# A graph layer: columns of an on-chip x picked by VectorE for one of four gathers in each 16th run, with a sliding window of node sums

## The chip, the cores and the metric

The kernel runs on one core of a Trainium2 chip. All times are device microseconds of that core. The kernel before took 3992.48 us (median of three runs, 3992.14 to 3996.18). The profile is one more execution, taken by the hardware profiler.

## The reference

A graph with 12,500 nodes of 128 features and 412,500 edges, sorted by their destination. Features 0 to 31 are scalars, the other 96 are 32 vectors of three. For each edge an MLP of the 8 edge scalars gives four sets of 32 weights. The features of the source node are multiplied by the weights and by the edge's attributes, summed over the edges of each destination, projected, mixed with a product of the node's own features, added to x, and normalised along the features:

```python
f0 = x0 @ W1_0e / np.sqrt(MUL);  f1 = jnp.einsum('nui,uw->nwi', x1, W1_1o) / np.sqrt(MUL)
feat0, self0 = f0[:, :MUL], f0[:, MUL:];  feat1, self1 = f1[:, :MUL], f1[:, MUL:]
e0, e1 = feat0[edge_src], feat1[edge_src]
h = gelu(gelu(ea8 @ W_mlp1 / np.sqrt(8)) @ W_mlp2 / np.sqrt(64))
w00, w01, w10, w11 = h @ Wp_00, h @ Wp_01, h @ Wp_10, h @ Wp_11
...
mid0, mid1 = ...
n0 = segment_sum(mid0, edge_dst) / np.sqrt(32);  n1 = segment_sum(mid1, edge_dst) / np.sqrt(32)
y0 = c * self0 + s * (n0 @ W2_0e / np.sqrt(64));  y1 = ...
out = layernorm(x + concatenate([y0, y1]))
```

## The kernel before

The edges are cut into 806 runs of 512 (four columns q of 128 edges each) and the runs into 202 chunks of four. The order of work is written out by hand in the main loop over s (lines 717 to 761) for TensorE, ScalarE, VectorE and SP. GpSimd has the gathers alone.

- Prologue (lines 673 to 716). Each of 25 groups of 512 nodes is loaded, transposed into `acc` (`turn`, L187 to L192), multiplied by the feature weights `wf` (`features_of`, L194) and stored in DRAM as `table`. The first 16 runs don't wait for the table: they gather rows of x, which `turn_rows` (L414) and `features` (L422) turn into features on chip.
- `gather(s)` (L119 to L126). Four indexed DMAs on GpSimd, each bringing 128 rows of 512 bytes into `G[s]`. `G` has LEAD = 20 buffers, and the gathers of run s + 19 are issued in step s, so a gather waits until the messages 20 runs back have read their buffer.
- `aid(s, t)` (L108 to L117). In every 14th run from 36 on (55 runs) the last column isn't gathered by GpSimd: SP loads row numbers into registers, 16 at a time, and issues 128 single-row DMAs, beginning 16 steps ahead.
- `weights`, `mlp1`, `mlp2`, `radial`: the edge MLP on TensorE and ScalarE, a chunk at a time.
- `messages(s)` (L444, L447): VectorE multiplies the weights (in PSUM) by the gathered features into `M`. It stands in VectorE's order ahead of `placing(s)` (`pl`, L465), and in step 2 of a chunk ahead of `add`.
- `segments(s - 1)` (L456): TensorE sums the messages over up to 32 nodes of a column with the selection matrix `S` (`select`, L431 and L435, once a chunk). ScalarE copies the sums out (`sg`, L459).
- `place`, `project` (L472, L473, L481): TensorE puts the four runs of a chunk in node order and multiplies them by the output weights.
- `add(c)` (L485 to L490): VectorE loads four node numbers from `first_node` into registers and adds four 128x32 blocks to `acc` at those columns. `acc` holds all 12,500 nodes, transposed; it begins as x, so the residual is in it from the start.
- `self_part(b)` (L493 to L501): for each group, x is loaded again, transposed, multiplied by `ws` and added to `acc`. The 25 groups are spread over the first quarter of the loop.
- `norm(bs)` (`moments`, L506 to L524; `normalise`, L526 to L544): a group whose nodes are complete (`due`, L264 to L268) is transposed out of `acc`, normalised and stored.
- `general()` is a slow path for inputs that don't fit the fixed windows. It isn't entered for these inputs.

The lines on which the order around the change rests:

```python
G[s] = wk.tile([P, Q, P], F32, name="G", bufs=LEAD)
for q in range(Q - 1 if s in aided else Q):
...
if s + LEAD - 1 < NS:
    gather(s + LEAD - 1)
...
if 0 < s <= NS:
    segments(s - 1)
...
if s < NS:
    messages(s)
    placing(s)
```

Of the kernel before, what the change touches and what calls it, by code (L numbers as in the profile page):

```python
# [24 lines left out]
Q = 4  # L25
# [13 lines left out]
CATCH_UP = 46  # L39
MARGIN = 64  # L40
AID = 14
# [3 lines left out]
STEPS = 12  # L45
LNB = 2
# [3 lines left out]
def gnn_kernel(ctx: ExitStack, tc: tile.TileContext, x, src, dst, ea4, ea8, w1_0, w1_1, wm1, wm2,  # L50
# [44 lines left out]
    G, Y = {}, {}  # L95
    aided = range(AID_FROM, NS - 1, AID)
    assert AID_FROM >= raw_runs and AID_LEAD < LEAD and P % ROWS == 0 and STEPS <= AID
    assert len(aided) <= P

    aid_rows = cst.tile([max(len(aided), 1), P], I32)  # L100
    aid_at = cst.tile([max(len(aided), 1), P], I32)

    def aid_load():

        nc.sync.dma_start(aid_rows, sub(src, AID_FROM * SB + (Q - 1) * P, [[AID * SB, len(aided)], [1, P]]))
        nc.vector.tensor_scalar(aid_at, aid_rows, float(4 * P), None, op0=OP.mult)

# [11 lines left out]
    def gather(s):  # L119
        b, c = divmod(s, P)  # L120
        G[s] = wk.tile([P, Q, P], F32, name="G", bufs=LEAD)
        for q in range(Q - 1 if s in aided else Q):
            rows = idx_raw[:, s, q:q + 1] if s < raw_runs else idx[b][:, q, c:c + 1]
            nc.gpsimd.indirect_dma_start(  # L124
                out=G[s][:, q, :], out_offset=None, in_=x if s < raw_runs else table,
                in_offset=bass.IndirectOffsetOnAxis(ap=rows, axis=0))  # L126
# [14 lines left out]
    acc = cst.tile([P, N + W], F32)  # L141
# [45 lines left out]
    def turn(b):  # L187
        n0, nn, full, tail, tiles = group(b)
        PX[b] = ps.tile([P, GN], F32, name="w", bufs=CH)
        for t, k in tiles:  # L190
            nc.tensor.transpose(PX[b][:, t * P:t * P + k], XT[b][:k, t, :], ident[:k, :k])
        nc.scalar.activation(acc[:, n0:n0 + nn], PX[b][:, :nn], AF.Copy)  # L192

    def features_of(b):  # L194
        n0, nn, full, tail, tiles = group(b)
        pf = ps.tile([P, XB, P], F32, name="w", bufs=CH)
        for t, k in tiles:
            nc.tensor.matmul(pf[:k, t, :], acc[:, n0 + t * P:n0 + t * P + k], wf, start=True, stop=True)
        PF[b] = wk.tile([P, XB, P], F32, name="ft", bufs=3)
        if full:  # L200
            nc.vector.tensor_copy(PF[b][:, :full, :], pf[:, :full, :])
        if tail:
            nc.vector.tensor_copy(PF[b][:tail, full, :], pf[:tail, full, :])
# [15 lines left out]
    def clear():  # L219
        nc.vector.memset(wpost, 0.0)  # L220
        nc.vector.memset(acc[:, N:], 0.0)
        nc.vector.memset(ones, 1.0)
        nc.vector.memset(odd, 0.0)
# [20 lines left out]
    def make_ws():  # L244
        keep = math.cos(MIX) / math.sqrt(MUL)
        nc.vector.memset(ws, 0.0)
        nc.vector.tensor_scalar(ws[:MUL, :MUL], w1[:MUL, MUL:], keep, None, op0=OP.mult)
        nc.vector.scalar_tensor_tensor(ws[:, MUL:].rearrange("p (c i) -> p i c", i=3),
                                       comp[:, :, None].to_broadcast([P, 3, MUL]), keep,
                                       w1[:, None, MUL:].to_broadcast([P, 3, MUL]), op0=OP.mult, op1=OP.mult)  # L250

# [10 lines left out]
    self_from = min(raw_runs + CATCH_UP, NS // 4)  # L262
    self_every = max(1, (NS // 4) // NG)
    due = {}  # L264
    for b in range(NG):
        c = math.ceil((min((b + 1) * GN, N) + MARGIN) / N * NCH) - 1
        c = max(c, (self_from + self_every * (b + 1)) // CH)
        due.setdefault(min(c, NCH - 1), []).append(b)  # L268
    floor = cst.tile([1, NS], F32)

    def set_floor():
        nc.vector.memset(floor, 0.0)
        for c, bs in due.items():
            if (c + 1) * CH < NS:
                nc.vector.memset(floor[:, (c + 1) * CH:], float((bs[-1] + 1) * GN))

# [206 lines left out]
    def add(c):  # L483
        ns = min(CH, NS - c * CH)
        _, at = nc.values_load_multi_w_load_instructions(  # L485
            first_node[0:1, c * CH:c * CH + ns], engines=[DVE], min_val=0, max_val=N - 1,
            skip_runtime_bounds_check_because="node numbers")
        for k in range(ns):
            a = acc[:, bass.ds(at[k], W)]
            nc.vector.tensor_tensor(a, PC[c][:, k, :], a, op=OP.add)  # L490

    def self_part(b, xt):
        n0, nn, full, tail, tiles = group(b)  # L493
        pt = ps.tile([P, GN], F32, name="m", bufs=1)
        for t, k in tiles:
            nc.tensor.transpose(pt[:, t * P:t * P + k], xt[:k, t, :], ident[:k, :k])
        xs = wk.tile([P, GN], F32, name="xs", bufs=1)
        nc.scalar.activation(xs[:, :nn], pt[:, :nn], AF.Copy)
        pf = ps.tile([P, GN], F32, name="h")
        nc.tensor.matmul(pf[:, :nn], ws, xs[:, :nn], start=True, stop=True)  # L500
        nc.vector.tensor_tensor(acc[:, n0:n0 + nn], pf[:, :nn], acc[:, n0:n0 + nn], op=OP.add)  # L501
# [4 lines left out]
    def moments(b):  # L506
# [8 lines left out]
        st = wk.tile([P, XB, 6], F32, name="bst")  # L515
        for t, k in tiles:
            nc.tensor.transpose(pt[:k, t, :], acc[:, n0 + t * P:n0 + t * P + k], ident)
# [29 lines left out]
    def norm(bs, last=False):  # L547
        for b in bs:
            moments(b)
            if len(pend) == LNB:  # L550
# [5 lines left out]
    def general():  # L556
        T = max(t for t in range(1, P + 1) if E % t == 0)
        weight = dr.tile([NS, SB], F32)
        sums = dr.tile([N + P, P], F32)
        for b in range(NB):  # L560
            ns = min(P, NS - b * P)
            raw = load_run_rows(dst, b, NO_NODE)
            f = wk.tile([P, SB], F32, name="rawf")
            g = wk.tile([P, SB], F32, name="rawr", bufs=1)
            nc.vector.tensor_copy(f[:ns, :], raw[:ns, :])
            against_window(f, g, ns)
            nc.vector.tensor_scalar(f[:ns, :], g[:ns, :], 0.0, None, op0=OP.is_lt)
            nc.vector.tensor_scalar(g[:ns, :], g[:ns, :], J - 0.5, None, op0=OP.is_ge)
            nc.vector.tensor_tensor(f[:ns, :], f[:ns, :], g[:ns, :], op=OP.add)
            nc.sync.dma_start(weight[b * P:b * P + ns, :], f[:ns, :])  # L570
# [10 lines left out]
        wcol = weight.rearrange("s e -> (s e)")[:E].rearrange("(n t) -> t n", t=T)  # L581
# [4 lines left out]
        with tc.For_i(0, E // T, 1) as i:  # L586
            si = wk.tile([T, 1], I32, name="g_si")
            di = wk.tile([T, 1], I32, name="g_di")
            we = wk.tile([T, 1], F32, name="g_we")
# [4 lines left out]
            nc.sync.dma_start(we, wcol[:, bass.ds(i, 1)])  # L594
            nc.sync.dma_start(a4, r4[:, bass.ds(i, 1), :].rearrange("t n k -> t (n k)"))
            nc.sync.dma_start(a8, r8[:, bass.ds(i, 1), :].rearrange("t n k -> t (n k)"))
            g = wk.tile([T, P], F32, name="g_g", bufs=1)
            nc.gpsimd.indirect_dma_start(out=g, out_offset=None, in_=table,
                                         in_offset=bass.IndirectOffsetOnAxis(ap=si, axis=0))
            nc.vector.tensor_scalar(a4, a4, we, None, op0=OP.mult)  # L600
            p0 = ps.tile([RAD, T], F32, name="m", bufs=1)
            nc.tensor.transpose(p0, a8, ident[:T, :T])
            t8 = wk.tile([RAD, T], F32, name="g_t8", bufs=1)
# [3 lines left out]
            h1 = wk.tile([HID, T], F32, name="g_h1", bufs=1)  # L607
# [3 lines left out]
            h2 = wk.tile([HID, T], F32, name="g_h2", bufs=1)  # L611
# [3 lines left out]
            w = wk.tile([T, P], F32, name="g_w", bufs=1)  # L615
            nc.scalar.activation(w, pw, AF.Copy)

            m = wk.tile([T, 4, P], F32, name="g_m", bufs=1)
# [14 lines left out]
            mt = wk.tile([P, 4, P], F32, name="g_mt", bufs=1)  # L633
# [4 lines left out]
            y = wk.tile([T, P], F32, name="g_y", bufs=1)  # L638
# [6 lines left out]
            eq = wk.tile([T, T], F32, name="g_eq", bufs=1)  # L645
# [3 lines left out]
            eb = wk.tile([T, T], F32, name="g_eb", bufs=1)  # L649
# [6 lines left out]
            old = wk.tile([T, P], F32, name="g_old", bufs=1)  # L656
            nc.gpsimd.indirect_dma_start(out=old, out_offset=None, in_=sums,
                                         in_offset=bass.IndirectOffsetOnAxis(ap=di, axis=0))
            new = wk.tile([T, P], F32, name="g_new", bufs=1)
# [3 lines left out]
        for b in range(NG):  # L663
            n0, nn, full, tail, tiles = group(b)
            xt = load_nodes(b, sums)
            pt = ps.tile([P, GN], F32, name="m", bufs=1)
            for t, k in tiles:
                nc.tensor.transpose(pt[:, t * P:t * P + k], xt[:k, t, :], ident[:k, :k])
            nc.vector.tensor_tensor(acc[:, n0:n0 + nn], pt[:, :nn], acc[:, n0:n0 + nn], op=OP.add)
        norm(range(NG), last=True)  # L670

    with tc.manual_schedule(engines={PE, ACT, DVE, SP}):
# [35 lines left out]
        selfs, loaded = list(range(NG)), {}  # L708
# [7 lines left out]
        set_floor()  # L716
        for s in range(NS + 1 + CH):
# [13 lines left out]
            if k == 0 and c + 1 < NCH:  # L731
                mlp2(c + 1)
# [8 lines left out]
            if 0 < s <= NS:  # L741
                segments(s - 1)
            if k == 1 and 0 < c <= NCH:
# [13 lines left out]
            if selfs and s + 8 >= self_from and (s + 8) % self_every == 0:  # L757
                b = selfs.pop(0)
                loaded[s + 8] = b, load_nodes(b)
            if s in loaded:  # L760
                self_part(*loaded.pop(s))
        assert not selfs and not loaded


    late = cst.tile([1, NS], F32)
    nc.vector.tensor_copy(late, first_node)
    nc.vector.tensor_tensor(late, late, floor, op=OP.is_lt)
    nc.vector.tensor_reduce(odd[0:1, 2 * NB:], late, axis=mybir.AxisListType.X, op=OP.add)
# [35 lines left out]
```

## Time and profile before

| what | value |
|---|---|
| median of the timed runs | 3992.48 us |
| the profiled execution, its own time | 6014.41 us |
| its span, first to last instruction | 6012.6 us |
| TensorE clock granted, mean | 0.671 |
| TensorE busy | 3220.7 us (54%) |
| GpSimd busy | 2992.1 us (50%) |
| VectorE busy | 1693.3 us (28%) |
| ScalarE busy | 1024.6 us (17%) |
| gathers issued by GpSimd | 3105 from the table, 64 from x |
| single-row DMAs issued by SP | 7040 |
| packets in the span | 1,011,283 (265.85 MB, 44 GB/s) |

The profiled execution is 2022 us longer than the timed ones, so its shares of busy time are not those of a timed run. The table of groups gives, for each line of code and kind of instruction, the count, the busy time, the mean of one in ns, and the idle time of its engine just before it with what ended most of it. "PE" is TensorE, "PEld" its weight loads, "DVE" VectorE, "ACT" ScalarE, "POOL" GpSimd; a "q" behind the name is that engine's sequencer. The timeline gives start and length in us, engine, line, operation and tiles, and in brackets the idle time before it and what ended it. "remote" stands for a release that the profile can't name, "issue" for no wait that it shows.

### The profile page before, as it was taken

To read this page: it belongs to the slowest core of one execution; us is meant where nothing else is said; L and a number is where in the kernel's file an instruction comes from. 1 tells how busy PE (TensorE), PEld (TensorE's weight loads), DVE (VectorE), ACT (ScalarE), POOL (GpSimd) and SP (SyncE) were. 2 spreads that over 40 slices of the span, in tenths; PEclk is the share of its full clock that TensorE was granted. 3 is DMA by queue.
4 is the path that set the end of the run, shared out by engine and by line. 5 is a ranking of instruction groups with operands and counts; after the bars stand their busy time and mean duration, and the time that the engine had idled before them with its cause. 6 is when DMAs were issued, how large, how long until landed. Compare 5 with 4: busy or idle time off the path is not lost.

```text
span 6012.6 us, 82144 instructions
## 1 busy us (share of the span) xinstructions
PE 3220.7 (54%) x25199; PEld 2267.2 (38%) x25199; DVE 1693.3 (28%) x4943; ACT 1024.6 (17%) x2262; POOL 2992.1 (50%) x3176
## 2 busy tenths in 40 slices
PE   3654555555556555555555454545465455555446
PEld 3433433343334333333433333334343333343334
DVE  2322322222322222322222232222233222232223
ACT  1211111121111111111111111112112111111112
POOL 4555444544445545554554455454555555455552
PEclk6766666666766666666666666666666666666667
DMA  5222222222222222222222222222222222222221
GB/s 123 45 40 47 42 46 45 43 49 47 44 48 43 42 41 46 41 42 40 39 40 43 43 40 44 40 42 42 44 40 43 42 40 43 41 41 41 43 41 23
DMA packets 1011283, 265.85 MB, mean 44 GB/s; under 512 B 901422, under 2 KB 958519, under 8 KB 1010833
## 3 DMA queue, kind: packets, MB, share of 16 engines
q0 software_dynamic: 101408, 207.89, 13.4%
q1 hardware_dynamic: 889167, 46.16, 9.2%
q10 hardware_dynamic: 20258, 6.46, 0.4%
q8 instruction: 201, 3.29, 0.2%
q14 instruction: 249, 2.04, 0.1%
HBM read 247.45 MB, written 12.80 MB: 43 GB/s over the span
## 4 chain that ended last, share of the span: by engine, by line
PE 24%; another core or an unknown queue 23%; issue 5%; ACT 5%; DVE 2%; SPq 0%; DVEq 0%; DMA 0%; ACTq 0%
PE seg L456 4%; PE w L405 4%; PE m L473 4%; PE m L481 4%; PE m L472 3%; PE h L388 3%; PE h L373 2%; ACT h L393 1%; ACT h L377 1%; ACT sg L459 1%; ACT y L542 0%; PE m L364 0%; DVE M L447 0%; DVE acc L490 0%
## 5 line engine op out<-in xcount | busy, mean ns | idle before, releaser
L124 POOL DMA_INDIRECT G<-table,idx x3105 | 2930.6, 944 | 2910.9 <-DVE pl L465 1470.7
L456 PE MATMUL seg<-M,S 128*32 128x256 f32 x6448 | 667.5, 491 | 1845.4 <-ACT sg L459 1479.0
L465 DVE TENSOR_SCALAR pl<-iota,colv 128x128 f32<-128x128 f32 x806 | 227.2, 282 | 2441.6 <-PE m L473 2181.3
L456 PEld LDWEIGHTS seg<-M,S 128*32 128x32 f32 x6448 | 144.1, 122 | 2008.9 <-ACT sg L459 1526.5
L459 ACT ACTIVATE sg<-seg 128x256 f32<-128x256 f32 x806 | 310.6, 385 | 3143.1 <-remote 1978.9
L447 DVE TENSOR_TENSOR M<-w,G 128x384 f32<-128x384 f32 x1580 | 798.6, 547 | 0.0
L405 PE MATMUL w<-wpb,h 64*128 64x128 f32 x6448 | 693.5, 373 | 16.1 <-issue 15.9
L405 PEld LDWEIGHTS w<-wpb,h 64*128 64x128 f32 x6448 | 588.6, 267 | 154.8 <-issue 151.0
L388 PE MATMUL h<-h,w2b 64*64 64x256 f32 x3232 | 365.4, 473 | 351.8 <-ACT h L377 318.1
L473 PE MATMUL m<-pl,sg 128*128 128x96 f32 x1612 | 550.0, 442 | 0.0
L481 PE MATMUL m<-st,wpost 128*128 128x128 f32 (+1 forms) x1616 | 388.9, 416 | 146.9 <-ACT st L475 133.2
L472 PEld LDWEIGHTS m<-pl,sg 128*128 128x128 f32 x1612 | 404.8, 308 | 164.6 <-issue 117.0
L490 DVE TENSOR_TENSOR acc<-m,acc 128x32 f32 x806 | 154.5, 192 | 1072.8 <-PE m L481 402.4
L472 PE MATMUL m<-pl,sg 128*128 128x32 f32 x1612 | 424.3, 355 | 10.7 <-ACT eT L366 5.9
L473 PEld LDWEIGHTS m<-pl,sg 128*128 128x128 f32 x1612 | 413.3, 314 | 0.0
L481 PEld LDWEIGHTS m<-st,wpost 128*128 128x128 f32 x1616 | 335.8, 308 | 192.8 <-ACT st L475 141.7
L444 DVE TENSOR_TENSOR M<-w,G 128x256 f32<-128x256 f32 x790 | 330.3, 418 | 227.2 <-remote 218.2
L388 PEld LDWEIGHTS h<-h,w2b 64*64 64x64 f32 x3232 | 159.8, 158 | 542.1 <-ACT h L377 456.1
L393 ACT ACTIVATE h<-h 128x512 f32<-128x512 f32 x404 | 226.6, 595 | 523.9 <-PE h L388 242.2
L373 PE MATMUL h<-eT,w1b 64*128 64x128 f32 x3232 | 278.8, 311 | 28.7 <-issue 22.2
L373 PEld LDWEIGHTS h<-eT,w1b 64*128 64x128 f32 x3232 | 233.4, 213 | 145.3 <-issue 137.5
L377 ACT ACTIVATE h<-h 128x512 f32<-128x512 f32 x404 | 220.1, 596 | 368.9 <-remote 291.3
(105 smaller groups left out, 1162.5 us busy)
## 6 DMA issues: line engine op xcount, KB each, us to landing
G<-table SPq DMA_DIRECT2D x7040, 0.5 KB
G<-table,idx POOLq DMA_INDIRECT x3105
e<-in_edge_attr SPq DMA_DIRECT2D x201, 64.0 KB
xt<-in_x SPq DMA_DIRECT2D x48, 256.0 KB
e<-in_edge_attr SPq DMA_DIRECT2D x201, 32.0 KB
table<-ft ACTq DMA_DIRECT2D x24, 256.0 KB
out<-y SPq DMA_DIRECT2D x24, 256.0 KB
raw<-in_dst SPq DMA_DIRECT2D x6, 256.0 KB
```

What stands on the lines that cost most here:

```text
L124: nc.gpsimd.indirect_dma_start(out=G[s][:, q, :], out_offset=None, in_=x if s < raw_runs else table, in_offset=bass.IndirectOffsetOnAxis(a ...
L373: nc.tensor.matmul(p1[h][:, j // 2, j % 2, :], w1b[rows, j, :], eT[c][rows, :], start=True, stop=True)
L388: nc.tensor.matmul(p2[r][k * HID:(k + 1) * HID, h * n:(h + 1) * n], w2b[rows, :], H1[c][h][rows, k * n:(k + 1) * n], start=True, stop=True)
L393: nc.scalar.activation(H2[c][r].rearrange("p k j e -> p (k j e)"), p2[r], AF.Gelu_apprx_tanh, scale=1.0 / math.sqrt(HID))
L405: nc.tensor.matmul(WP[i][:, q, :], H2[c][q % 2][rows, k, q // 2, :], wpb[rows, :], start=True, stop=True)
L444: nc.vector.tensor_tensor(m[:, :, :, :MUL], w[:, :, :2 * MUL].rearrange("p q (a u) -> p q a u", a=2), g[:, :, None, :MUL].to_broadcast([P, ...
L447: nc.vector.tensor_tensor(m[:, :, j, MUL:].rearrange("p q (i u) -> p q i u", i=3), w[:, :, None, (2 + j) * MUL:(3 + j) * MUL].to_broadcast ...
L456: nc.tensor.matmul(pt[q * W:(q + 1) * W, :], S[c][:, r * Q + q].rearrange("p k j -> p (k j)"), M[s][:, q].rearrange("p a u -> p (a u)"), s ...
L459: nc.scalar.activation(SG[s], pt, AF.Copy)
L472: nc.tensor.matmul(pt[:, k, :W], SG[s][:, :P], PL[s][:, :W], start=True, stop=True)
L473: nc.tensor.matmul(pt[:, k, W:], SG[s][:, P:], PL[s][:, W:], start=True, stop=True)
L481: nc.tensor.matmul(PC[c][:, :ns, :], wpost[:, k, :], ST[c][:, :ns, k, :], start=k == 0, stop=k == 3)
```

## The change

- `acc` becomes `xT`: the transposed x stays on chip unchanged through the whole kernel.
- The node sums are kept in a window of ACC = 768 nodes, two buffers from a pool. After a group is normalised, `next_sums` takes a new window: a memset of the last 512 columns on VectorE and a copy of the other 256 from the old one on ScalarE. `find_first` computes once, before the loop, where in its window each run's first node lies (`first_at`), and `add` uses that. The end counts the runs that lie outside (`strays`).
- `self_part` and its loads are gone. `ws` gets the identity added, so that xT times `ws` is the own term and the residual together; `moments` forms it in PSUM (`stop=False`) and adds the sums to it by a second product with the identity. The spreading of the groups over the first quarter (`CATCH_UP`, `self_from`) goes too, so groups 0 and 1 are due in chunks 9 and 17 where they were due in 17 and 19; all others stay.
- In every 16th run from 40 on (48 runs) GpSimd doesn't gather column 2. Instead VectorE loads the source numbers into registers, eight at a time, and copies single columns of `xT` into `GT[s]` (`pick`): one batch of eight in each step, from 18 to 3 steps ahead of the run. Two steps ahead, `picked_rows` multiplies `GT[s]` by `wf` on TensorE, and ScalarE copies the product into `G[s]`.
- `mlp2` of the next chunk moves from before `weights` to behind `segments(s - 1)`.
- `general()` now sums all edges itself and borrows buffers from `G`; it isn't entered for these inputs.

```diff
-CATCH_UP = 46
+ACC = 768
+COLS = 16
+COL_ROWS = 8
...
+    picked = {DVE: range(AID_FROM + 4, NS - 1, COLS)}
...
+        for e, r in picked.items():
+            nc.sync.dma_start(pick_rows[e], sub(src, r[0] * SB + (Q - 2) * P, [[COLS * SB, len(r)], [1, P]]))
+
+    def pick(e, s, t):
+
+        if t == 0:
+            GT[s] = wk.tile([P, P], F32, name=f"gt{list(picked).index(e)}")
+        i = picked[e].index(s)
+        r0, r1 = t * COL_ROWS, (t + 1) * COL_ROWS
+        _, r = nc.values_load_multi_w_load_instructions(
+            pick_rows[e][i:i + 1, r0:r1], engines=[e], min_val=0, max_val=N - 1,
+            skip_runtime_bounds_check_because="node numbers")
+        for k in range(r1 - r0):
+            to, of = GT[s][:, r0 + k:r0 + k + 1], xT[:, bass.ds(r[k], 1)]
+            if e == DVE:
+                nc.vector.tensor_copy(to, of)
+            else:
+                nc.scalar.activation(to, of, AF.Copy)
+
+    def picked_rows(s):
+
+        pt = ps.tile([P, P], F32, name="m", bufs=1)
+        nc.tensor.matmul(pt, GT[s], wf, start=True, stop=True)
+        nc.scalar.activation(G[s][:, Q - 2, :], pt, AF.Copy)
...
-        for q in range(Q - 1 if s in aided else Q):
+        for q in range(Q):
+            if q == Q - 1 and s in aided or q == Q - 2 and any(s in r for r in picked.values()):
+                continue
...
-    acc = cst.tile([P, N + W], F32)
+    xT = cst.tile([P, N], F32)
...
+        nc.vector.tensor_tensor(ws, ws, ident, op=OP.add)
...
+    def find_first():
+
         nc.vector.memset(floor, 0.0)
         for c, bs in due.items():
             if (c + 1) * CH < NS:
                 nc.vector.memset(floor[:, (c + 1) * CH:], float((bs[-1] + 1) * GN))
+        nc.vector.tensor_tensor(floor, first_node, floor, op=OP.subtract)
+        nc.vector.tensor_scalar(strays, floor, 0.0, float(ACC - W), op0=OP.max, op1=OP.min)
+        nc.vector.tensor_copy(first_at, strays)
+        nc.vector.tensor_tensor(strays, strays, floor, op=OP.not_equal)
+
+    def next_sums(old=None):
+        A["now"] = wk.tile([P, ACC], F32, name="acc")
+        if old is None:
+            nc.vector.memset(A["now"], 0.0)
+        else:
+            nc.vector.memset(A["now"][:, ACC - GN:], 0.0)
+            nc.scalar.activation(A["now"][:, :ACC - GN], old[:, GN:], AF.Copy)
...
         for t, k in tiles:
-            nc.tensor.transpose(pt[:k, t, :], acc[:, n0 + t * P:n0 + t * P + k], ident)
+            nc.tensor.matmul(pt[:k, t, :], xT[:, n0 + t * P:n0 + t * P + k], ws, start=True, stop=sums is not None)
+            if sums is None:
+                nc.tensor.matmul(pt[:k, t, :], A["now"][:, at + t * P:at + t * P + k], ident,
+                                 start=False, stop=True)
+            else:
+                nc.vector.tensor_tensor(pt[:k, t, :], pt[:k, t, :], sums[:k, t, :], op=OP.add)
...
-            if k == 0 and c + 1 < NCH:
-                mlp2(c + 1)
+            for e, runs in picked.items():
+                for t in range(P // COL_ROWS):
+                    if s + 2 + P // COL_ROWS - t in runs:
+                        pick(e, s + 2 + P // COL_ROWS - t, t)
+                if s + 2 in runs:
+                    picked_rows(s + 2)
...
             if 0 < s <= NS:
                 segments(s - 1)
+            if k == 0 and c + 1 < NCH:
+                mlp2(c + 1)
...
-            if selfs and s + 8 >= self_from and (s + 8) % self_every == 0:
-                b = selfs.pop(0)
-                loaded[s + 8] = b, load_nodes(b)
-            if s in loaded:
-                self_part(*loaded.pop(s))
```

## The prediction

> **What bounds the kernel now.** I read the page's table of groups first, then GpSimd's own timeline, then the table of waits, then the end of the trace.
>
> ```profile
> L124 POOL DMA_INDIRECT G<-table,idx x3105 | 2930.6, 944 | 2910.9 <-DVE pl L465 1470.7
> ```
> ```profile
> 3045.82 0.95 POOL L124 DMA_INDIRECT G<-table,idx  x1 [0.30 <-issue]
> 3047.08 0.94 POOL L124 DMA_INDIRECT G<-table,idx  x1 [0.30 <-issue]
> ...
> 3055.81 0.94 POOL L124 DMA_INDIRECT G<-table,idx  x1 [0.30 <-issue]
> ```
> The second view is GpSimd alone while nothing holds it. Eight steps take 3055.81 - 3045.82 = 9.99 us, so one gather costs 1.249 us: 0.944 busy and 0.30 between. There are 3105 gathers from the table and 64 from x, 3169 in all.
>
> The profiled execution took 6014.4 us (span 6012.6), the timed runs 3992.5. So the next thing to ask is what the profiled one does with 2022 us that the timed ones don't have. The table of waits:
> ```profile
> DVE pl L465 <- PE m L473: 2181.3, 171, 16.5
> ACT sg L459 <- remote: 1978.9, 202, 16.4
> ```
> Once in each four-run chunk (202 times) ScalarE stands before the `sg` copy up to 16.4 us for nothing that the trace names; TensorE and VectorE stand behind it, and GpSimd later, when its 20 buffers are used up. The sum against the profile's own time: 3.5 us to the first gather, 3168 steps x 1.249 = 3956.8, the last gather's 0.9, and 87.5 from its end (5925.1) to the span's end make 4048.7. The other 1963.9 of 6012.6 us is GpSimd idle beyond its 0.30 us steps, which is the size of the 1978.9 us of stalls. Without them the end of the kernel should look like this:
> ```profile
> 5924.19 0.95 POOL L124 DMA_INDIRECT G<-table,idx  x1 [0.31 <-issue]
> ...
> 5984.87 0.41 DVE L444 TENSOR_TENSOR M<-w,G 128x256 f32<-128x256 f32 x1
> ...
> 6003.09 0.80 SPq L166 DMA_DIRECT2D out<-y  x1
> ```
> The last run's messages start at 5984.87, 27.7 us before the end; the compute was some 60 us behind only through the stalls. A run without them: 3.5 + 3956.8 + 0.9 + about 2 for the landing + 27.7 + 1.8 around the span = 3992.7, against a median of 3992.5. So I take the timed runs to be paced by GpSimd's gathers from first to last, with no stall that reaches it. That is an inference: the timed runs have no trace.
>
> How far is the compute from that pace? Chunks that catch up at the end, with all data there, show it (stage windows; columns are length, PE, PEld, DVE, ACT, POOL busy, clock, DMA):
> ```profile
> 5939.30:5950.20 10.90, 10.48 (x123) 7.19 (x123) 7.66 (x24) 4.37 (x10) 0.00 (x0) 1.00 0.06 2
> ```
> A chunk takes 10.9 us at clock 1.00, with VectorE busy 7.66. GpSimd needs 16 gathers less 4/14 for aided runs, 15.71 x 1.249 = 19.6 us. So 8.7 us of each chunk is free on the compute side.
>
> [...] the trace's one-column form (DVE_READ_ACCUMULATOR) took 83 ns and 128x8 forms 166[...] The trace shows hardly any such contention even for `pl` (L465, 128 columns, SBUF to SBUF): the 280 unheld gather steps that overlap one average 1249.5 ns, 2075 steps beside no VectorE work 1248.4.
>
> **The change, part by part.**
>
> *Gathers removed.* 48 runs (40, 56, ... 792) lose one gather of four; the built order has 3057 + 64 = 3121. 48 x 1.249 = 59.95 us, all of it on GpSimd's path: -59.9.
>
> *Column picks added to VectorE.* 768 batches, one in each run from 22 to 789, each a register load of 8 values and 8 pairs of register operation and 128x1 copy. The trace has none of these copies. Load: 343 ns for 4 values on VectorE's sequencer (L485), 1236 for 16 on SP (L112); 8 lie between, I take 0.69 us, 0.34 at best (if it hides under the queued messages, as L485 did at 3032.79). Copy: the register operation alone takes 69 ns (L490), the one-column form 83; the `acc` adds, same register addressing, repeat every 0.227 us (0.87 for four), which is the dear end. I take 0.115 each. A batch is 0.69 + 0.92 = 1.6 us, between 0.34 + 0.66 = 1.0 and 0.69 + 1.82 = 2.5; a chunk has four, 6.4 (4.0 to 10.0). They stand ahead of messages(s), so the messages, `pl`, the adds and TensorE's segments wait behind them. Put wholly in series the chunk becomes 10.9 + 6.4 = 17.3 us; GpSimd's new pace is (16 - 4/14 - 4/16) x 1.249 = 19.3. Cost on the path: 0, covered by 2.0 us a chunk even in series; the dear end is the rival below.
>
> *picked_rows.* 48 products 128x128 (two passes of some 0.34) and 48 ScalarE copies of 0.27, two runs ahead of use; hidden under the same slack: 0.
>
> *self_part removed, moments changed.* Away: 25 loads on SP, 98 transposes, 50 passes of 1.07, a ScalarE copy (0.58) and a VectorE add (0.69) for each group. Added: for 98 tiles four passes (0.34 each) where one transpose was, a 512-column memset (0.49) and a 128x256 ScalarE copy (0.39) for 24 groups. All in the slack except for the last group, two tiles: 8 passes where 2 transposes were, in the tail, about +0.7 with their overlap (0 to 2).
>
> *mlp2 moved behind segments.* TensorE no longer meets the wait for the GELU before the segments: 0 under slack.
>
> *Prologue.* find_first adds two 1x806 operations of about 1 us (L767 took 0.98), a copy and the first sums' memset, less two that ran early before: about +2.7 us ahead of messages(0), and one more load on SP. In the trace GpSimd waits on turn_rows (PE h L414: 30.4 us, 13 times) in the raw runs, so this may show once: 0 to +4, I take +1.
>
> *VectorE beside GpSimd.* Two copies fall in each gather. As dear as an L465: 2 x 1.1 ns x 3121 = 7 us[...]. I take +0.7, 0 to +7. A gain is excluded in each of these three, since nothing is taken from those paths.
>
> *Sum.* -59.9 + 0.7 + 1.0 + 0.7 = -57.5. On the timed median 3992.5: 3935. On the profile's own 6014.4 I expect less to be seen, as its end is set by the stalls, which stay.
>
> **The rivals.**
>
> *VectorE becomes the pace (slower).* At 2.5 us a batch and in series, a chunk takes 10.9 + 10.0 = 20.9 us, 1.6 over the gathers, through 192 chunks: 307 us, so 3933 + 307 = 4240. It decides from 2.1 us a batch ((19.3 - 10.9)/4). For it: no cover but slack, every batch ahead of messages. Against: VectorE idles 3.2 us of 10.9, where part of the batch fits, and the sequencer loads registers while the engine works.
>
> *SP's queue becomes the pace.* The aided rows: 33 issues in 14.35 us with two register loads (SP timeline at 3030), 0.435 each, 128 in 14 runs: 55.7, with edge loads some 60, of 68.7 us before and 67.6 after. But the issue rows also last up to 1.4 us when held, and I can't tell how much of that the timed runs have. If SP had no slack before, only its 25 loads (0.5 us each) go: 3980.
>
> *GpSimd is slowed by the copies.* A gather that is held by two whole copies (2 x 83 ns) would lengthen 3121 steps by 0.17 us: much slower. The L465 numbers speak against it; I count it with the slower case. A mild form, 10 ns a step, gives 3966.
>
> That the gathers stay is excluded by the built order.
>
> **Chances.** Forecast 0.78, its own range 3929 to 3947 (all ends added); mild contention or partial waits 0.06 (3947 to 3984); SP 0.07 (half of it within 0.2%); VectorE or GpSimd slowed 0.09. A range of 3928 to 3966 leaves under 0.2 out. By 0.2%, about 8 us and about what a measurement of this kernel can tell from no change: faster 0.87, same 0.04, slower 0.09.
>
> **What would show it.** Gathers 3121 at 1.249 us unheld, also beside the copies; batches of 1.6 us on VectorE; catch-up chunks still below 19.3 us; aided rows landed before their messages. The prediction is wrong if unheld steps lengthen, if a batch passes 2.1 us, or if catch-up chunks take longer than the gathers.

## The result, and the profile after

| | median | lowest and highest | runs |
|---|---|---|---|
| before | 3992.53 us | 3992.14 to 3996.18 | 4 |
| after | 3934.52 us | 3934.11 to 3935.08 | 4 |

The ratio is 0.9853, with a 95% interval of 0.9836 to 0.987: 58.0 us less, where the prediction had 57.5 less and 3935. The profiled execution of the changed kernel took 3934.22 us (span 3932.4), so it is like the timed ones and can be read directly. That is not so for the one of before that the prediction had to read (6014.4 us).

First the table of groups. The columns after the bar are the busy time and the mean of one in ns, then the idle time before them and what ended most of it.

```profile
L156 POOL DMA_INDIRECT G<-table,idx x3057 | 2887.8, 945 | 934.3 <-issue 835.4
...
L492 DVE TENSOR_TENSOR M<-w,G 128x256 f32<-128x256 f32 x790 | 334.9, 424 | 1063.9 <-DMA G<-table,idx 900.2
...
L128 DVE COPY gt<-xT 128x1 f32 x6144 | 620.8, 151 | 171.4 <-issue 151.6
```

GpSimd has 3057 + 64 = 3121 gathers where it had 3169. Its idle time of 934.3 us is the 0.30 us between one gather and the next and little else: 12 of the 3120 steps are longer than 1.35 us, 4.2 us too long in all, more than half of it in one wait of 2.5 us for the first part of the table; and 835.4 of the 934.3 is "issue", no wait that the profile shows. VectorE, on the other hand, stands 900.2 us in all before the first product of its messages until a gather has landed. That is how this kernel looks when its gathers pace it: the engine that issues them never waits, and the reader waits for their data. The same in the table of waits (total in us, how often, longest in us):

```profile
DVE M L492 <- DMA G<-table,idx: 900.2, 436, 5.9
POOL G L156 <- issue: 854.3, 2802, 0.3
```

The two largest waits of before, `DVE pl <- PE m` and `ACT sg <- remote`, were the stalls of that one execution. Both are gone; VectorE now waits for gathers, and the row of GpSimd has nothing over the 0.3 us of its step.

The end of the kernel, on three engines:

```profile
3904.35 0.94 POOL L156 DMA_INDIRECT G<-table,idx  x1 [0.30 <-issue]
```
```profile
3908.55 0.42 DVE L492 TENSOR_TENSOR M<-w,G 128x256 f32<-128x256 f32 x1 [4.18 <-DMA G<-table,idx]
```
```profile
3925.69 1.42 SPq L198 DMA_DIRECT2D out<-y  x1
```

The last gather starts at 3904.35; the last run's messages start 4.2 us later, as soon as it has landed, 3.3 us after its own end where the prediction's sum has about 2; the rest is the tail. From the first gather (3.52) to the last, 3120 steps took 3900.83 us, 1.2503 each.

VectorE's picks, two of its batches. The second is 8 copies in 0.96 us, with the register load visible ahead of it as 0.62 us of idle time:

```profile
2001.39 0.96 DVE L128 COPY gt<-xT 128x1 f32 x8 [0.51 <-issue]
...
2005.61 0.96 DVE L128 COPY gt<-xT 128x1 f32 x8 [0.62 <-issue]
2006.62 0.42 DVE L492 TENSOR_TENSOR M<-w,G 128x256 f32<-128x256 f32 x1
...
2017.60 0.42 DVE L492 TENSOR_TENSOR M<-w,G 128x256 f32<-128x256 f32 x1 [2.10 <-DMA G<-table,idx]
```

0.62 + 0.96 = 1.6 us for a batch whose load isn't hidden. Over all 768 batches the table of groups gives less: (620.8 + 171.4) / 768 = 1.03 us of VectorE for one, idle time included, since much of the loading runs while the engine still works: 375 of the 467 us that the 768 loads take. At 2017.60 the messages wait 2.10 us for a gather although a batch stood ahead of them: in that run the picks cost nothing.

### The profile page after: what moved, and what is told of

It reads as the page before. It is cut to its first block, busy times and chain, and to the rows that moved or that the text cites. A ratio compares the mean times of both kernels' runs of the same rounds, so it can differ in the third digit from the quotient of the medians.

```text
span 3932.4 us, 95859 instructions
## 1 busy us (share of the span) xinstructions
PE 2866.2 (73%) x25441; PEld 1990.8 (51%) x25441; DVE 2310.2 (59%) x11089; ACT 1021.0 (26%) x2309; POOL 2949.3 (75%) x3128
## 4 chain that ended last, share of the span: by engine, by line
POOL 31%; issue 23%; DMA 14%; PE 12%; DVE 9%; SPq 7%; ACT 3%; DVEq 1%; POOLq 0%; ACTq 0%
POOL G L156 31%; DMA G<-table,idx 12%; SPq L146 5%; DVE M L495 3%; PE w L453 3%; PE m L529 2%; PE seg L504 1%; SPq L142 1%; PE h L436 1%; PE m L521 1%; DVE M L492 1%; DVE acc L538 1%; PE m L520 1%; DVE gt L128 1%; DMA xt<-in_x 1%
## 5 line engine op out<-in xcount | busy, mean ns | idle before, releaser
L156 POOL DMA_INDIRECT G<-table,idx x3057 | 2887.8, 945 | 934.3 <-issue 835.4
L453 PE MATMUL w<-wpb,h 64*128 64x128 f32 x6448 | 773.8, 349 | 632.8 <-DVE M L495 632.4
L492 DVE TENSOR_TENSOR M<-w,G 128x256 f32<-128x256 f32 x790 | 334.9, 424 | 1063.9 <-DMA G<-table,idx 900.2
L504 PE MATMUL seg<-M,S 128*32 128x256 f32 x6448 | 618.9, 461 | 181.4 <-DVE M L495 134.5
L128 DVE COPY gt<-xT 128x1 f32 x6144 | 620.8, 151 | 171.4 <-issue 151.6
L521 PE MATMUL m<-pl,sg 128*128 128x96 f32 x1612 | 387.9, 325 | 0.0
L520 PEld LDWEIGHTS m<-pl,sg 128*128 128x128 f32 x1612 | 269.1, 210 | 143.2 <-ACT eT L414 119.0
L520 PE MATMUL m<-pl,sg 128*128 128x32 f32 x1612 | 306.5, 274 | 35.5 <-ACT eT L414 34.1
L436 PE MATMUL h<-h,w2b 64*64 64x256 f32 x3232 | 322.8, 534 | 0.0
L529 PE MATMUL m<-st,wpost 128*128 128x128 f32 (+1 forms) x1616 | 317.0, 357 | 1.2 <-ACT st L523 1.2
L529 PEld LDWEIGHTS m<-st,wpost 128*128 128x128 f32 x1616 | 270.6, 254 | 34.0 <-issue 18.0
L521 PEld LDWEIGHTS m<-pl,sg 128*128 128x128 f32 x1612 | 272.5, 212 | 0.0
```

What stands on the lines that cost most here:

```text
L128: nc.vector.tensor_copy(to, of)
L156: nc.gpsimd.indirect_dma_start(out=G[s][:, q, :], out_offset=None, in_=x if s < raw_runs else table, in_offset=bass.IndirectOffsetOnAxis(a ...
L436: nc.tensor.matmul(p2[r][k * HID:(k + 1) * HID, h * n:(h + 1) * n], w2b[rows, :], H1[c][h][rows, k * n:(k + 1) * n], start=True, stop=True)
L453: nc.tensor.matmul(WP[i][:, q, :], H2[c][q % 2][rows, k, q // 2, :], wpb[rows, :], start=True, stop=True)
L492: nc.vector.tensor_tensor(m[:, :, :, :MUL], w[:, :, :2 * MUL].rearrange("p q (a u) -> p q a u", a=2), g[:, :, None, :MUL].to_broadcast([P, ...
L504: nc.tensor.matmul(pt[q * W:(q + 1) * W, :], S[c][:, r * Q + q].rearrange("p k j -> p (k j)"), M[s][:, q].rearrange("p a u -> p (a u)"), s ...
```

## The experiments

Two theories stood at the beginning. The first is the prediction's: GpSimd's gathers are the pace from first to last, so a gather removed is worth 1.25 us, and all else in the change lies in slack. The rival says that the gain comes from elsewhere too (the reloads of x that are gone, the moved `mlp2`, the own term as a product), or that the picks cost part of what the gathers give.

### The kernel before once more

No edit: `before.py` again, to get an execution of it that looks like the timed ones.

> The kernel before, profiled once more. Theory (GpSimd's gathers pace it): in an execution whose own time is that of the timed runs, 3169 gathers follow each other every 1.249 to 1.251 us, GpSimd's idle time beyond the 0.30 us steps is under 10 us, and VectorE waits for gathers to land. Rival (something else paces the timed runs and the fit of the sum is chance): GpSimd waits for buffers, tens of us or more beyond its steps.

It took 3997.05 us, span 3995.3, without the stalls. The table of waits of this run:

```profile
ACT sg L459 <- PE seg L456: 1778.9, 601, 8.2
DVE M L444 <- DMA G<-table,idx: 1647.3, 577, 6.0
POOL G L124 <- issue: 884.5, 2900, 0.3
```

The line `ACT sg <- remote`, 1978.9 us in the first profile, is gone, and what is left is the picture that the prediction inferred: VectorE waits 1647.3 us for gathers, and only 7 of GpSimd's 3168 steps are longer than 1.35 us, 3.3 us too long in all, inside the 10 us of the expectation. The first gather started at 3.57, the last at 3967.24; 3168 steps of 1.2512; then 28.1 us to the end. With the change VectorE waits 1647.3 - 900.2 = 747.1 us less.

### The gathers back, the rest of the change kept

```diff
-    picked = {DVE: range(AID_FROM + 4, NS - 1, COLS)}
+    picked = {}
```

> The changed kernel without picked runs: GpSimd gathers all four columns again (3169), everything else of the change stays (x transposed on chip, window of sums, own term as a product, mlp2 later). Theory: the gathers are the whole gain, so the time goes back to 3992 to 3995. Rival (the dropped self term, its 25 loads of 256 KB and the moved mlp2 carry part of the gain): 3950 to 3985.

3996.54 us (3993.07 to 4000.33, 13 runs), ratio to the kernel before 1.0008, interval 0.9999 to 1.0016. That is 1.5 us above the range of the theory and far from the rival's 3950 to 3985. So the window of sums, the own term as a product, the reloads that are gone and the moved `mlp2` together gain nothing that can be measured; if anything they cost some 3 us. The whole gain hangs on the picks, that is on the 48 gathers. VectorE's wait in this run:

```profile
DVE M L491 <- DMA G<-table,idx: 1562.0, 533, 11.1
```

So of the 747.1 us of waiting that are gone, 85 go with the rest of the change and 661.8 with the picks, 0.86 us for each of the 768 batches.

### Picks of fixed columns

One copy of eight fixed columns takes the place of each batch, which leaves out the choice of the source nodes. The work of all other engines stays.

```diff
-        _, r = nc.values_load_multi_w_load_instructions(
...
+        nc.vector.tensor_copy(GT[s][:, r0:r1], xT[:, r0:r1])
```

> The changed kernel with each batch of a register load, eight register operations and eight single-column copies replaced by one copy of eight columns at a fixed place; this leaves out the choice of the source nodes for the picked column. 3121 gathers as in the changed kernel. Theory: the picks lie wholly beside GpSimd's gathers, so 3932 to 3935. Rival (the 6144 small copies hold GpSimd's steps up, or delay the messages): 3900 to 3928.

3935.38 us (3931.03 to 3936.49, 4 runs), ratio 0.985 (0.9835 to 0.9865), against 0.9853 for the changed kernel. That is 0.4 us above the theory's 3932 to 3935, and the rival, a gain of 7 us or more, is out. VectorE's wait for gathers rises from 900.2 to 1365.7 us, and the time stays:

```profile
DVE M L484 <- DMA G<-table,idx: 1365.7, 498, 6.1
```

What the picks need, they take from waiting time. Their cost on the path is zero within what these runs can tell apart.

### Every copy twice

Sixteen copies in a batch instead of eight.

```diff
-                nc.vector.tensor_copy(to, of)
+                for _ in range(2):
+                    nc.vector.tensor_copy(to, of)
```

> The changed kernel with every single-column copy made twice: a batch grows from 1.6 to about 2.5 us of VectorE. Theory: VectorE still waits for gathers some 1.1 us a run in the changed kernel (900 us in its table of waits over 806 runs), and the second copies need 0.92 us a run, so it just fits: 3934 to 3950. Rival (batches add to the chunk in series, limit 2.1 us a batch, as the prediction's slower case has it): 10.9 + 4 x 2.5 = 20.9 us a chunk, about 4240.

4052.45 us (4043.41 to 4054.83, 4 runs), ratio 1.0149 (1.0133 to 1.0164). Neither expectation held: the slack doesn't cover it, and the cost is far from that of a pure series. A batch of VectorE in this run, and then GpSimd's waits for buffers and VectorE's for gathers:

```profile
2001.35 2.40 DVE L129 COPY gt<-xT 128x1 f32 x16 [0.61 <-issue]
2003.77 0.42 DVE L493 TENSOR_TENSOR M<-w,G 128x256 f32<-128x256 f32 x1
```
```profile
POOL G L157 <- DVE gt L129: 151.7, 400, 7.4
DVE M L493 <- DMA G<-table,idx: 4.9, 13, 0.4
```

Of those 151.7 us, 400 x 0.30 are the step that every gather has; a step of 7.4 us is one that no run above shows. With 2.4 us of copies and up to 0.6 of load, the messages hardly wait for gathers any more (4.9 us). In all, GpSimd is held 49 times, for 59 us in all, because the messages that free its buffers come late, and the tail after the last gather grows from 28 to 82 us: the compute is some 54 us behind when the gathers are done. In the changed kernel the longer steps came to 4, so 59 - 4 + 54 = 109, and between the two profiled executions the time rose by 4043.4 - 3934.2 = 109. By the medians it is 118, 0.6 us a chunk. VectorE is the pace here: it is 82% busy and waits some 40 us for TensorE's sums.

### More different picks: every 12th run and every 8th

The doubled copies write the same column twice, so their price needn't be that of more picks. Two kernels make more real ones, 16 in a batch.

```diff
-COLS = 16
-COL_ROWS = 8
+COLS = 12
+COL_ROWS = 16
```

> The changed kernel with COLS = 12 and COL_ROWS = 16: 64 runs instead of 48 lose a gather to VectorE's picks (3105 gathers), 16 columns a batch, 8 batches in 12 runs. Per chunk of four runs VectorE does 42.7 copies instead of 32. Theory (picks lie in VectorE's slack): 16 x 1.25 = 20 us less, 3914.5, range 3911 to 3920. Rival (VectorE is already near the pace, as the run with doubled copies suggests: it held at 19.7 us a chunk with 2.5 to 3.0 us a run): batches of 16 take about 1.2 us of load and 1.85 us of copies, 2.0 us a run on average; where two or three of them follow each other the messages come late and the ring of 20 buffers has to cover it; 3925 to 3960 then.

3914.33 us (3911.41 to 3915.93, 4 runs), ratio 0.9806 (0.9789 to 0.9822): the 3914.5 of the theory. VectorE still waits 501.3 us for gathers. A batch of 16 costs it 2.43 us on average, load included, and two runs of three have one: 1.6 us a run.

With `COLS = 8` every run has a batch of 16:

> The changed kernel with COLS = 8 and COL_ROWS = 16: 96 runs lose a gather to VectorE's picks (3073 gathers), 16 different columns in every run instead of 8. If picks at twice the number still lie in slack: 96 - 48 = 48 gathers less, 60 us, 3874.5. Theory now (the doubled copies showed that VectorE becomes the pace above some 2.4 us a run): a batch is 1.2 us of load, part of it hidden, and 16 x 0.115 = 1.85 us of copies, 2.4 to 3.1 us a run; a chunk then takes 19.7 us or more against GpSimd's 19.0: 4000 to 4300, slower than the changed kernel. Wholly in series it is 10.9 + 12.4 = 23.3 us a chunk, about 4700.

3963.32 us (3945.4 to 3978.81, 6 runs, which lie further apart than those of the other kernels), ratio 0.9932 (0.9906 to 0.9958). It gives 29 us of the gain back instead of adding 60, which is the direction of the theory, but its 4000 to 4300 was too dear. VectorE in this run, two of the four runs of a chunk:

```profile
2003.19 1.87 DVE L128 COPY gt<-xT 128x1 f32 x16 [0.61 <-issue]
2005.14 0.42 DVE L492 TENSOR_TENSOR M<-w,G 128x256 f32<-128x256 f32 x1
...
2010.33 1.83 DVE L128 COPY gt<-xT 128x1 f32 x16
2012.20 0.42 DVE L492 TENSOR_TENSOR M<-w,G 128x256 f32<-128x256 f32 x1
```

The first batch shows 0.61 us of its load, the second none: a load of 16 values takes 1.127 us (the median of the 768 in this run), and VectorE is at work without a pause from 2008.86 until the batch. These two use 1.83 and 2.5 us, the mean of all is 2.40 a run, VectorE never waits over 0.4 us for a row, and a chunk takes 3958.0 / 202 = 19.6 us, against 19.0 that the 15.2 gathers need. GpSimd hardly notices: its longer steps come to 13 us, and its last gather starts at 3853.7. But 104 us follow after that, where the changed kernel has 28: the 20 buffers let the messages fall behind the gathers, and the lag is paid at the end.

### ScalarE picks as well

ScalarE makes the same copies for 48 other runs, eight in a batch.

```diff
-    picked = {DVE: range(AID_FROM + 4, NS - 1, COLS)}
+    picked = {DVE: range(AID_FROM + 4, NS - 1, COLS), ACT: range(AID_FROM + 12, NS - 1, COLS)}
```

> The changed kernel, with ScalarE making the same column picks for another 48 runs (one of each 16, eight columns a batch, each an ACT copy of 128x1): 3073 gathers. Theory (GpSimd is the only pace, ScalarE is busy 26%): 48 x 1.25 = 60 us less, 3874.5, range 3871 to 3885. Rival (ScalarE is late in TensorE's chain: the copies of sg, w and st wait behind 8 picks of some 0.2 us and a register load of 0.6, about 2.2 us a run or 9 us a chunk on top of 5 us busy): ScalarE or TensorE behind it becomes the pace, 3934 or more, up to 4200.

3878.89 us (3877.37 to 3882.0, 4 runs), ratio 0.9717 (0.9701 to 0.9734). The theory holds for a second engine too. ScalarE is 42% busy instead of 26%, and VectorE still waits 675.9 us for gathers.

The last step was to put both together, with `COLS` and `COL_ROWS` for each engine: VectorE every 12th run with batches of 16, ScalarE every 16th with batches of 8.

> VectorE's picks of every 12th run (16 columns a batch) together with ScalarE's picks of every 16th (8 a batch): 112 runs lose a gather, 3057 are left. Theory (GpSimd's gathers are the pace as long as every other queue keeps up): 16 gathers fewer than with ScalarE's and VectorE's picks of every 16th, 20 us below its 3879: 3859, range 3855 to 3866. Rival (the two sets of picks add up in the chain from VectorE over TensorE to ScalarE): 3870 to 3950.

3866.81 us (3864.11 to 3868.73, 4 runs), beside 4001.49 for the kernel before in the same series: ratio 0.9663, interval 0.9647 to 0.9679. In us it ends just above the theory's range, but the kernel before was 8 us longer in this series than in that of ScalarE's first version; by the ratios the step from ScalarE's first version is 0.56%, 21.6 us for 16 gathers. This is the fastest version of the study, 1.9% below the changed kernel by the ratios. VectorE's wait for gathers is down to 80.9 us, so little is left to take:

```profile
DVE acc L539 <- PE m L530: 309.7, 123, 5.6
DVE pl L514 <- PE m L522: 147.4, 58, 7.8
DVE M L493 <- DMA G<-table,idx: 80.9, 52, 4.1
```

### Where ScalarE ends it

Batches of 16 on both engines, each for every 12th run:

> Both engines pick for every 12th run, 16 columns a batch: 128 runs lose a gather, 3041 are left. Theory: 32 gathers fewer than with both at every 16th: 3879 - 40 = 3839, range 3835 to 3847. Rival: ScalarE's batch of 16 (a load of 1.2 us and 16 copies of 0.2, some 4 us) stands ahead of sg and w's copies and the chain from TensorE to VectorE becomes the pace: 3860 to 4000.

4191.74 us (4185.24 to 4195.14, 4 runs), ratio 1.0472 (1.0455 to 1.0489): the rival's side, and beyond its range. In TensorE's waits the third line is one that the runs above don't have:

```profile
PE w L454 <- DVE M L496: 300.1, 73, 7.0
PE m L521 <- ACT eT L415: 295.2, 195, 2.7
PE m L136 <- DVE S L484: 272.0, 61, 8.6
```

L136 is the product of `picked_rows`. ScalarE's picked runs began at 46 here, so its product stood in step 0 of a chunk, right behind `select`, and the two share the one PSUM buffer `m`. Was that the cause? The same kernel with ScalarE's runs one earlier:

```diff
-    picked = {DVE: range(AID_FROM + 4, NS - 1, COLS[DVE]), ACT: range(AID_FROM + 10, NS - 1, COLS[ACT])}
+    picked = {DVE: range(AID_FROM + 4, NS - 1, COLS[DVE]), ACT: range(AID_FROM + 9, NS - 1, COLS[ACT])}
```

> As the run with both engines at every 12th, but ScalarE's picked runs start at 45 instead of 46, so that their products stand in step 3 of a chunk instead of step 0. In step 0 the product shares TensorE's one PSUM buffer m with select, which VectorE has just written: 61 waits, 272 us. Theory A (this place is what made 4192): the waits go, 3041 gathers are the pace, 3839 to 3860. Theory B (ScalarE's batches of 16 in series with the rest are what made it): 4150 to 4200 again, with the 272 us of waits turned into others. If both count, 3870 to 4100.

4140.62 us (4131.51 to 4150.02, 4 runs), ratio 1.0368 (1.0346 to 1.039). The 272 us of waits are gone, and by the ratios the time falls by 1.0%, 41 us (51 by the medians, but the kernel before was 7 us shorter in this series): the place was a small part. The larger part, about 300 us over the 3839 that the gathers would allow, stays, so theory A falls; theory B's range was missed by 9 us, and its side is the nearer one. ScalarE in this run:

```profile
2010.52 1.07 ACT L426 ACTIVATE h<-h 128x512 f32<-128x512 f32 x2
2011.48 0.39 ACT L508 ACTIVATE sg<-seg 128x256 f32<-128x256 f32 x1
2011.85 1.67 ACT L131 ACTIVATE gt<-xT 128x1 f32 x16
2014.85 0.39 ACT L508 ACTIVATE sg<-seg 128x256 f32<-128x256 f32 x1 [1.33 <-PE seg L505]
```

A batch is 1.67 us of copies behind a load of 1.05, and `sg`, `eT` and `st` stand behind it in ScalarE's order; TensorE waits 242 us for `eT` and 118 for `sg`. From the fastest version this kernel differs in ScalarE's picks alone, so the rise of 274 us between the two (281 by the ratios) comes with these, on top of VectorE's. ScalarE's batches of 16 without VectorE's weren't run. A further point on the same side is ScalarE at every 8th run:

> VectorE picks for every 12th run, ScalarE for every 8th, 16 columns in each run: 159 runs lose a gather, 3010 are left. If gathers are still the pace: 3879 - 63 x 1.25 = 3800. Theory now: ScalarE gets some 4 us more in each run, 16 us a chunk on top of 5 us busy, 21 us against GpSimd's 18.7 a chunk, so ScalarE becomes the pace: 4000 to 4400. SP's queue is the other candidate: one aided run in 14 takes it some 59 us of the 65.5 us that 14 runs then last, with 6 us left for edge loads and results: 3810 to 3850 if only that counts.

4229.54 us (4226.69 to 4234.07, 4 runs), ratio 1.0566 (1.0548 to 1.0583), in the range of the theory, but not by its reason, which had ScalarE full: ScalarE is 54% busy, no engine over 75%, and VectorE, TensorE and ScalarE each wait for another. That fits a chain from VectorE over TensorE to ScalarE and back that sets the pace; no run tests it.

### SP's queue

The prediction's rival was that SP is the pace. It is tested from the other side, with more work for SP and less for GpSimd.

```diff
-AID = 14
+AID = 12
```

> The changed kernel with AID = 12 instead of 14: 64 runs instead of 55 get their fourth set of rows from SP's single-row copies, so GpSimd does 9 gathers fewer (3112 instead of 3121), and SP issues 9 x 136 instructions more, 128 rows in 12 runs instead of 14. Theory (GpSimd's gathers are the pace, SP has slack): 9 x 1.25 = 11 us less, 3923, range 3920 to 3928. Rival (SP's queue is close to the pace): the rows of an aided run come late, TensorE and VectorE wait for them and hold GpSimd; no gain, 3934 or more, up to 4000.

4077.63 us (4074.96 to 4081.06, 4 runs), ratio 1.0211 (1.0194 to 1.0228). The expectation counted 64 aided runs; there are 65, ten more than the 55, and so ten gathers fewer. They cost 143 us, more than the rival's 4000 allowed. The rows that SP issued, and its timeline, rows of the aided runs with the edge loads between them:

```profile
L146 SPq DMA_DIRECT2D G<-table x8320: 227/228/340, 182.4 to 4050.2; - x199
```

```profile
2004.29 18.73 SPq L146 DMA_DIRECT2D G<-table  x48
2023.13 1.47 SPq L403 DMA_DIRECT2D e<-in_edge_attr  x2
2026.24 11.80 SPq L146 DMA_DIRECT2D G<-table  x32
2038.14 1.62 SPq L403 DMA_DIRECT2D e<-in_edge_attr  x2
2041.18 18.71 SPq L146 DMA_DIRECT2D G<-table  x48
```

There is no gap but the loads of 16 register values (1.25 us each, the median in the changed kernel). From 200 to 3800 us SP's pauses of 0.5 us or more come to 4.5 us in all; in the changed kernel they come to 303. Near the end VectorE waits for the rows that SP still issues:

```profile
4051.82 0.42 DVE L492 TENSOR_TENSOR M<-w,G 128x256 f32<-128x256 f32 x1 [16.98 <-DMA G<-table]
```

The 128 rows of an aided run take SP 53.3 us, loads and short gaps included, in this run and in the changed kernel alike; with the edge loads and the few others between them a period takes 59.6 us (7731 rows from 200 to 3800 us). Twelve runs at GpSimd's pace (3900.8 / 806 = 4.84 us) last 58.1. So at 12 SP needs more than GpSimd gives it, and it sets the pace to the end: 8320 rows are 65 aided runs, from 182.4 to 4050.2 they take 59.5 us each, and after the last row 29 us of 4079.3 are left. At 14 a period has 67.8 us for an estimated 61 (53.3 and 14/12 of the other 6.3). That SP has slack, as the first theory said, is true of the changed kernel and no longer so two runs closer.

## Why the prediction was right, point by point

All gains beside the gathers removed, each against the kernel before of the same series:

| picks by | gathers fewer | time less | of each gather |
|---|---|---|---|
| VectorE, every 16th (the change) | 48 | 58.0 us | 1.21 us |
| VectorE, every 12th | 64 | 79.1 | 1.24 |
| VectorE and ScalarE, every 16th | 96 | 114.5 | 1.19 |
| VectorE every 12th, ScalarE every 16th | 112 | 134.7 | 1.20 |

- *Gathers removed, -59.9.* Right. The steps between the two unstalled profiles fell from 3963.7 to 3900.8 us, 62.8, of which 48 x 1.25 = 60 are the gathers; the other 3 are the scatter of the mean step (1250.1 and 1248.9 ns for the steps under 1.35 us). The inference under it, that the timed runs are paced by GpSimd while the profile shows 6014 us, was the risky part, and the second profile of before confirms it.
- *Picks, 1.6 us a batch, 0 on the path.* The zero is right: the fixed columns ran at the same time. The 1.6 us is right only where the load shows (0.62 + 0.96); the mean is 1.03, the prediction's cheap end, and the picks took 0.86 us of waiting each. The 10.9 us to which the prediction added them is off the other way. It was read at a granted clock of 1.00 with TensorE busy 10.48 us; from 1000 to 3000 us the changed kernel was granted 0.79 to 0.80, and TensorE was busy 73%, 14.1 us of a chunk of 19.3. So the 2.0 us of cover are not shown as a number, only that there was enough: 900.2 us of waiting were left.
- *picked_rows, self_part, moments, mlp2: 0.* Right as a sum: 1.0008 (0.9999 to 1.0016) with the picks taken out. None of them was tried alone.
- *Tail, +0.7.* Not seen: 28.05 us from the start of the last gather to the span's end, 28.06 before.
- *Prologue, +1.0.* Not seen. GpSimd's one long step at the first table gather took 3.48 us after the change and 3.66 before. So of the 2.4 us that the sum adds back, none is seen at its place. That the total came within half a microsecond of 58.0 is luck; the median of the kernel before moved between 3992.5 and 4001.5 from series to series.
- *VectorE beside GpSimd, +0.7.* Nothing that stands out. The 1227 gather steps that overlap a pick average 1249.97 ns, the 589 beside no VectorE work at all 1248.54: 1.43 ns x 1227 = 1.8 us, less than the two profiles differ by themselves; 0.6 of the 1.4 ns are six single steps over 1.35 us. The 1.1 ns that the prediction read for L465 hangs on such single steps too: without the steps over 1.35 us the profile of before has 1248.4 beside L465 and 1248.3 elsewhere. The prediction took 0.115 us for a one-column copy; the profile has 151 ns from start to end, but in most batches one every 0.115 us, and the pace of the series is what counts in the sum.
- *The rival "VectorE becomes the pace".* It didn't happen at 1.6 us a batch. Its point, 2.1 us a batch, fits the runs: at 1.6 us a run (every 12th) VectorE still waited 501 us for gathers, at 2.40 (every 8th) no longer. Its price was wrong: at 2.5 us it had 20.9 us a chunk and 4240 us, and the runs with 2.40 and 2.63 on average took 3963 and 4052. Put in series, a batch costs its whole time; in the trace of the changed kernel 375 of the 467 us of loads run while VectorE works.
- *The rivals "SP's queue" and "GpSimd slowed".* Both absent in the changed kernel. SP waited 297 us for results to store there; its 55.7 us for an aided run, read in the stalled profile, is 53.3, and its "some 60" with the edge loads is some 61. It was nearer to the edge than a chance of 7% sounds: two runs closer together and it decides.

## What to carry to other kernels

When one engine issues without a wait and its reader waits for the data, an instruction taken off it was worth nearly its whole step here (1.19 to 1.24 of 1.25 us), and work added to the reader was free as long as it still waited for that data (466 us less of waiting in the changed kernel than with fixed columns, at 3934.5 and 3935.4 us). That wait, 1647 us before, 900 after, 81 in the fastest version, tells what is left; work for another engine in the chain, as ScalarE's, isn't measured by it. Before a queue that is off the path is given more, sum its work for one period and set it against the period: SP's some 60 us fitted in the 67.8 us of 14 runs and not in the 58.1 of 12. A profile that is much longer than the timed runs can still be used if the stall is named, its sum explains the difference and the rest adds up to the timed median.

## What the runs showed of the hardware

- The profiled execution of the kernel before took 6014.4 us, with 202 waits of up to 16.4 us that no trace line explains; the same kernel profiled again took 3997.05 without any of them. What caused them stays open.
- A copy of one column, addressed by a register, took 151 ns on VectorE (the mean of 6144 in the changed kernel) and came every 0.114 us in a row ((1.87 - 0.154) / 15, every 8th run); with each made twice to the same column, every 0.150 on average ((2.40 - 0.15) / 15). The register operations ahead of the copies came every 0.115 us in the changed kernel. In 272 of its 768 batches, most with six of the eight register operations done before the first copy, the copies came every 0.061 us, and a batch of eight took as little as 0.51 us. On ScalarE a copy took 191 ns (the median of 8192, both engines at every 12th) and came every 0.099 us ((1.67 - 0.19) / 15, the same with ScalarE's runs one earlier), faster than on VectorE.
- Loading 8 register values took 606 ns on VectorE (the changed kernel) and 553 on ScalarE (the fastest version), loading 16 took 1125 and 1047 (both engines at every 12th); all four are medians.
